# The last sequence's score comparison on GpSimd and ScalarE, and the last block's output in two halves

## The chip, the cores and the metric

The kernel runs on one core of one Trainium2 chip. The metric is the device time of one execution in microseconds. Three runs of the kernel before took 418.65, 418.74 and 420.13 us; the median is 418.74. One more execution was taken by the profiler: it took 417.93 us, of which 416.2 us are the span from the first instruction to the last. All times "at" a moment below are us from the start of that span.

## What is computed

Two layers over a batch of 4 sequences of 1024 rows of 128 numbers. Each layer computes `x = x + s * silu(g)` from the layer-normed `x`. In layer 0, `s` is a decayed linear attention and `g` a four-layer feed-forward network. In layer 1, `s` is a selective state space (a convolution, a gated scan over time with 16 states for each of the 128 channels, a projection) and `g` a mixture-of-depths network, which only the half of the rows with the highest router scores goes through:

```python
# layer 1, s
h = A_discrete[None] * h + xc_t[:, :, None] * B_t[:, None, :]
y = jnp.einsum('bn,bdn->bd', C_t, h) + D_param * xc_t
...
y = y * silu(gate)
y = y @ W_out + b_out
# layer 1, g
k = int(S * CAPACITY_FACTOR)                      # 512 of 1024
top_scores, top_idx = jax.lax.top_k(scores, k)
weights = jax.nn.sigmoid(top_scores)
...
output = jax.vmap(scatter_one)(hidden_states, top_idx, update)
```

The kernel has no sort: it counts for each row how many rows beat it, and keeps the rows that fewer than 512 beat.

## The kernel before

The rows are worked on in 8 blocks of 512 (`NBK`), two to a sequence, with the 128 channels in the partitions. A block goes through the stages `ln0`, `retention`, `gated`, `hidden1`, `hidden2`, `out0` (layer 0), then `ln1`, `front`, `states`, `gates`, `router`, `moe`, `scans`, `project` (layer 1). When both blocks of a sequence have their scores, `ranks(b)` runs for the sequence and `finish(j)` for each of its blocks.

Nothing is issued in the order in which it is written. Every instruction is recorded with a modelled cost and a priority (`TIMES` gives each stage of each block a start), and a list planner, `Plan.order`, decides the order of each engine once, before the launch. `Plan.issue` (line 373) then emits everything, so that line stands at every instruction of the profile and groups are told apart by tile names. On the chip each engine runs its list in that fixed order: an instruction whose input is late holds up all behind it on its engine. SyncE's list (SP in the profile) issues all DMAs.

The steps that the change touches:

- `scans` (lines 921 to 956). For each of 8 double tiles `u` of a block (128x2x512): two DMAs fetch rows of `xd` into `u`; VectorE (DVE) multiplies by `B` (128x1024) and runs two scans (128x512 each); GpSimd (POOL) multiplies by `Cr` (line 950; the very last tile on VectorE); TensorE (PE) sums the states with `sel` into `py`. Tiles are named `u_block_k`; in the last block they come in the order u_7_0, u_7_8, u_7_1, u_7_9, u_7_2, u_7_10, u_7_3, u_7_11, and the first two get their rows from TensorE (`pu`, four products) in place of DMAs. The tag `u` has 6 buffers (line 422).
- `ranks` (lines 891 to 919). For each of 8 chunks `q`, VectorE compares the scores `sc` from that chunk on (n = 1024, 896, ... 128 columns) with the chunk's own scores `col` and adds up the results in the same instruction (lines 907 to 909); a second one, `eq` (line 910), settles ties. TensorE sums `cmp` and `eq` over the partitions into `rank` (lines 911 to 915). `cmp` and `eq` have two buffers each, so chunk q + 2 waits until TensorE has read chunk q. `wm` (router weight or 0) comes out at the end and scales `ff` in `finish`.
- `project` (lines 958 to 969). VectorE makes `y` from `py`, `xc` and `gate`; TensorE multiplies by `W_out`, chunk by chunk, and adds the bias last; ScalarE (ACT) copies the sum `pyo` to `so`.
- `finish` (lines 971 to 982). ScalarE scales `ff`, GpSimd adds `xn`, ScalarE applies silu; then `so * ff`, `x +` that, and the store. In the last block VectorE does the last two.
- The weights `w12_t` (line 591, used by `gated`) and `h_t` (line 596, used by `hidden1` and `hidden2`) have memory of their own to the end.

Of the kernel before, what the change touches and what calls it, by code (L numbers as in the profile page):

```python
# [47 lines left out]
for _name, _w in (  # L48
# [9 lines left out]


TIMES = {  # L60
    "ln0": (10.465, (-34.463, 37.568, 0.307, -8.702, 29.140, 25.837, -0.706, 2.276)),
    "retention": (7.697, (19.747, 29.540, 0.054, 5.261, 0.588, -0.481, 27.669, 17.510)),
    "gated": (0.198, (17.080, -12.778, -2.899, 37.127, 52.075, 3.684, 35.848, 24.681)),
    "hidden1": (181979.521, (10.669, -0.997, 0.654, 26.140, 49.753, 13.692, 29.323, 21.440)),
    "hidden2": (104.604, (6.706, 7.824, 35.607, 17.363, 7.255, 8.335, 12.787, 23.305)),
    "out0": (0.269, (-10.144, 10.621, 13.685, 32.888, 37.354, 6.208, 14.587, 34.725)),
    "ln1": (0.086, (-3.447, -9.822, 3.389, 39.108, 24.646, 10.527, 7.924, 19.641)),
    "front": (99775.310, (31.104, -7.375, 49.241, 35.721, 3.625, 15.911, 8.435, 28.268)),
    "states": (1929558528.870, (-22.925, -12.719, -2.927, -2.692, -1.385, 5.843, 8.364, 33.960)),
    "gates": (2802.502, (-10.124, -3.354, -1.683, 3.017, 7.752, 67.130, 11.212, 9.313)),  # L70
    "router": (35.459, (32.003, 36.047, 1.039, 23.096, 29.397, 12.314, 55.205, 9.245)),
    "moe": (0.850, (-6.037, 10.367, -2.942, 3.023, 8.714, 12.982, 45.904, 32.432)),
    "ranks": (3.658, (7.924, -5.386, 32.363, 0.750, 18.387, 5.771, 15.184, 9.739)),
    "scans": (0.083, (26.879, 6.452, 3.058, 25.041, 26.277, 9.568, 13.774, 14.948)),
    "project": (0.218, (-2.585, 1.221, 6.521, 8.046, 9.527, 12.283, 10.650, 21.658)),
    "finish": (2311.973, (10.042, -1.800, 14.285, 18.479, 29.156, 18.433, 18.474, 24.699)),
    "load_x": (0.107, (32.705, -1.570, 6.609, 55.729, 2.835, 7.712, 33.265, 51.716)),
}
SWITCH = 0.725
SPARE = 2  # L80
XB = 5
BY_PE = (0, NBK - 1)
U_BY_PE = (NBK - 1,)
# [298 lines left out]
def tile_kernel(  # L382
# [34 lines left out]
    for name, n in {  # L417
        "x": XB, "stat0": 2, "ve0": 2, "rs0": 2, "tm0": 2, "stat1": 2, "ve1": 2, "rs1": 2, "tm1": 2, "col": 2, "wm": 2, "most": 2, "eq": 2,
        "nxt": 2, "xn0": 2, "xnT": 1, "qT": 1, "vd": 1, "sT": 1, "st": 1, "y": 1,
        "sc": 1, "xh0": 2, "xl0": 2, "sO": 2, "xh1": 2, "xl1": 2, "Br": 1, "Cr": 2, "bc": 1,  # L420
        "gate": 2, "xc": 2, "cmp": 2, "a": 3, "xn1": 3, "ff": 3, "so": 3,
        "hh": 8, "hl": 8, "h2": 5, "u": 6, "last": 2,
    }.items():
        early = name in ("a", "h2")
        plan.tag(sb, name, n, early or name in ("hh", "hl", "u"), 1 if early else None)

    def tile_(tag, name, shape=(P, HB), dtype=F32):
        if tag == "const":
            tag = name
            plan.tag(sb, tag, 1)  # L430
        return plan.tile(tag, shape, dtype, name)
# [108 lines left out]
    def v(name, i=0, n=P):  # L540
        a = _VEC[name][0] + i
        return vec[0:n, a : a + 1]
# [5 lines left out]
    def c(name):  # L548
        a, b = _CST[name]
        return cs[:, a:b]  # L550
# [3 lines left out]
        return rw[:, a:b].repeat(n)  # L554

    ident = c("ident")
    ones_bf = tile_("const", "ones_bf", (P, 1), BF)
    do("gpsimd", "memset", ones_bf, 1.0, cost=0.05)
    zero = tile_("const", "zero", (P, 3))
# [28 lines left out]
    mm(pM, wqk[:, 0:D], wqk[:, D : 2 * D], True, True)  # L588
    M = split(pM, "M", (P, D))
    place(0.0)  # L590
    w12_t = tile_("const", "w12_t", (P, 2 * F), FR)
    vcopy(w12_t, w12_s)
    place(0.3)
    h_t = []
    for i, s in enumerate(h_s):
        h_t.append([tile_("const", f"h{i}_t{k}", (P, F), FR) for k in range(KC)])
        for k in range(KC):
            vcopy(h_t[i][k], s[k])
    place(0.5)
# [39 lines left out]
    two = tile_("const", "two", (P, P), FR)  # L639
    vcopy(two, two_s[:, 0:P])  # L640

    def add_bias(dst, i):

        mm(dst, two, bias[:, i * D : (i + 1) * D].repeat(CB), False, True)


    wr_s = tile_("sT", "wr", (P, P))
# [243 lines left out]
    def ranks(b):  # L891

        sc, col = prev["sc"], prev["col"]
        wm = tile_("wm", f"wm_{b}", (P, NCH))

        act(AF.Tanh, wm, col, scale=0.5)
        vts(wm, wm, 0.5, 0.5, ALU.mult, ALU.add)


        rank = mm_tile(f"rank_{b}", (P, NCH))  # L900
        most = tile_("most", f"most_{b}", (P, NCH))
        for q in range(NCH):
            n = L - q * P
            cmp = tile_("cmp", f"cmp_{b}_{q}", (P, L), BF)
            eq = tile_("eq", f"eq_{b}_{q}", (P, P), BF)
            cq = col[:, q : q + 1]
            do("vector", "tensor_scalar", cmp[:, 0:n], sc[:, q * P : L], cq, float(TOPK - n),
               op0=ALU.is_le, op1=ALU.add, accum_out=most[:, q : q + 1],
               cost=(n + 66) / 960 + 0.065)
            stt(eq, sc[:, q * P : (q + 1) * P], cq, tie, ALU.is_equal, ALU.mult)  # L910
            with fused("tensor", 0.027 * (NCH - q)):
                for i in range(q + 1, NCH):
                    mm(rank[:, i : i + 1], cmp[:, (i - q) * P : (i - q + 1) * P], ones_bf,
                       q == 0 and i == 1, False)
                mm(rank[:, q : q + 1], eq, ones_bf, False, q == NCH - 1)
        vtt(most, rank, most, ALU.is_lt)
        vtt(wm, wm, most, ALU.mult)
        for g in range(NH):
            R[b * NH + g]["wm"] = wm[:, g * CB : (g + 1) * CB]

    def scans(j):

        b, g = divmod(j, NH)
        xc, xd, Bp, Cr = (R[j][k] for k in ("xc", "xd", "B", "Cr"))
        py = tile_("py", f"py_{j}")
        last = prev.get("last")
        if not g:
            prev["last"] = tile_("last", f"last_{j}", (P, NSC))
        for m in range(4):
            us = []  # L930
            for q in range(0, 4, 2):
                ks = [4 * q + m, 4 * (q + 1) + m]
                u = tile_("u", f"u_{j}_{ks[0]}", (P, 2, HB))
                if m == 0 and j in U_BY_PE:
                    for i, k in enumerate(ks):
                        pu = mm_tile(f"pu_{j}_{k}")
                        mm(pu, rep[q + i], xc, True, True)
                        vtt(u[:, i, :], pu, R[j]["Br"], ALU.mult)
                else:
                    for i, k in enumerate(ks):  # L940
                        dma(u[:, i, :], xd[k * E : (k + 1) * E, :].whole(NS), 0.63, 2.24e5)
                    vtt(u, u, Bp.repeat(2), ALU.mult)
                for i, k in enumerate(ks):
                    do("vector", "tensor_tensor_scan", u[:, i, :], A[:, k : k + 1].bcast(HB),
                       u[:, i, :], last[:, 4 * m + q + i : 4 * m + q + i + 1] if g else 0.0, ALU.mult, ALU.add,
                       cost=(2 * HB + 104) / 960)
                if not g:
                    copy(prev["last"][:, 4 * m + q : 4 * m + q + 2], u[:, :, HB - 1])

                (vtt if j == NBK - 1 and m == 3 and q else ptt)(u, u, Cr.repeat(2), ALU.mult)  # L950
                us += [u[:, 0, :], u[:, 1, :]]
            with fused("tensor", 1.0):
                for q in range(4):
                    mm(py[32 * q : 32 * (q + 1), :], sel[:, 32 * m : 32 * (m + 1)], us[q],
                       m == 0, m == 3)
        R[j]["py"] = py

    def project(j):
        py = R[j]["py"]
        y = tile_("y", f"y_{j}")  # L960
        stt(py, R[j]["xc"], v("Dp"), py, ALU.mult, ALU.add)
        vtt(y, py, R[j]["gate"], ALU.mult)
        po = mm_tile(f"pyo_{j}", (P, CB, D))
        with fused("tensor", 1.15):
            for i, t in enumerate(chunk):
                mm(po[:, i, :], y[:, t], wout_t, i == 0, False)
            add_bias(po, 0)
        R[j]["so"] = so = tile_("so", f"so_{j}", (P, CB, D))
        copy(so.flat(), po.flat())

    def finish(j):
        b, g = divmod(j, NH)
        ff, xn, so, wm = (R[j][k] for k in ("ff", "xn1", "so", "wm"))
        for i in range(CB):
            act(AF.Copy, ff[:, i, :], ff[:, i, :], scale=wm[:, i : i + 1])
        ptt(ff, ff, xn, ALU.add)
        act(AF.Silu, ff, ff)
        xg = xts[j]
        tt = vtt if j == NBK - 1 else ptt
        tt(so, so, ff, ALU.mult)  # L980
        tt(xg, xg, so, ALU.add)
        dma(out[b, g * HB : (g + 1) * HB, :].rearrange("(c p) d -> p c d", p=P), xg)


    def stage(f, j, arg):
# [101 lines left out]
```

## Time and profile before

| | us |
|---|---|
| median of three runs (418.65 to 420.13) | 418.74 |
| the profiled execution | 417.93 |
| its span, first to last instruction | 416.2 |
| VectorE busy in the span | 354.4 |
| GpSimd busy | 288.1 |
| ScalarE busy | 276.3 |

The page of the profile gives busy times of the engines, then the span in 40 slices, then the chain of work that ended last, then the costliest groups. A timeline row reads: start, duration, engine, line, operation, output tile <- input tiles, shape, count; in brackets how long the engine had been idle before it and what ended that. "PEld" is TensorE's weight load, "SPq" a DMA's issue on SyncE's queue. A row with x4 covers four instructions in a row; instructions of VectorE overlap a little, so four scans of 1.26 us take 4.80.

The last block's work in order, from the timeline: `xc` of block 7 (convolution and silu) is written by ScalarE at 363.17 to 363.86. VectorE finishes the scans of block 6 at 366.1, does `ranks` of the last sequence from 366.01 on, and begins block 7's `u` at 374.73. TensorE's last product of the mixture network ends at 391.6. The page's 40 slices of 10.4 us each (busy share in tenths; the last row is the granted TensorE clock in tenths of full speed); the last five cover this stretch:

```
PE   1999999999999999999999999999999999989843
DVE  5594605996999968989999969999999999999992
ACT  3687895876557857875867598668577656772600
POOL 3066542198486897869996488967788898773890
PEclk9999999999999999999999999999999999998966
```

### The profile page before, as it was taken

To read this page: it belongs to the slowest core of one execution; us is meant where nothing else is said; L and a number is where in the kernel's file an instruction comes from. 1 tells how busy PE (TensorE), PEld (TensorE's weight loads), DVE (VectorE), ACT (ScalarE), POOL (GpSimd) and SP (SyncE) were. 2 spreads that over 40 slices of the span, in tenths; PEclk is the share of its full clock that TensorE was granted. 3 is DMA by queue.
4 is the path that set the end of the run, shared out by engine and by line. 5 is a ranking of instruction groups with operands and counts; after the bars stand their busy time and mean duration, and the time that the engine had idled before them with its cause. 6 is when DMAs were issued, how large, how long until landed. Compare 5 with 4: busy or idle time off the path is not lost.

```text
span 416.2 us, 6589 instructions
## 1 busy us (share of the span) xinstructions
PE 389.7 (94%) x2294; PEld 291.1 (70%) x2294; DVE 354.4 (85%) x621; ACT 276.3 (66%) x487; POOL 288.1 (69%) x200
## 2 busy tenths in 40 slices
PE   1999999999999999999999999999999999989843
PEld 1878878866777778777687688677877687747501
DVE  5594605996999968989999969999999999999992
ACT  3687895876557857875867598668577656772600
POOL 3066542198486897869996488967788898773890
PEclk9999999999999999999999999999999999998966
DMA  6900009206418053573602490456073553517300
GB/s 214 330 30 1 2 25 248 57 10 156 120 51 255 27 158 102 133 199 105 202 3 54 132 252 2 116 165 160 1 228 101 158 127 104 125 56 198 103 25 25
DMA packets 37897, 47.44 MB, mean 114 GB/s; under 512 B 7844, under 2 KB 17700, under 8 KB 37864
## 3 DMA queue, kind: packets, MB, share of 16 engines
q1 hardware_dynamic: 37864, 47.02, 40.8%
q8 instruction: 18, 0.29, 0.3%
q14 instruction: 15, 0.12, 0.1%
HBM read 42.40 MB, written 4.60 MB: 113 GB/s over the span
## 4 chain that ended last, share of the span: by engine, by line
PE 82%; DVE 5%; ACT 5%; POOL 4%; issue 2%; DMA 1%; POOLq 1%; SPq 1%; DVEq 0%; ACTq 0%
PE pb L373 15%; PE pa L373 12%; PE p L373 7%; PE py L373 7%; PE pg L373 6%; PE px L373 5%; PE pmo L373 5%; PE pm L373 4%; DVE u L373 4%; PE po L373 3%; POOL u L373 3%; PE pyo L373 2%; PE pv L373 2%; PE psc L373 2%; PE tr L373 2%
## 5 line engine op out<-in xcount | busy, mean ns | idle before, releaser
L373 POOL TENSOR_TENSOR u<-u,Cr 128x1024 f32<-128x1024 f32 x63 | 149.7, 2389 | 31.1 <-ACT last L373 13.0
L373 DVE TENSOR_TENSOR u<-u,B 128x1024 f32<-128x1024 f32 x62 | 73.5, 1206 | 17.1 <-DMA u<-xd 8.7
L373 DVE TENSOR_TENSOR_SCAN u<-bankA,last,u 128x512 f32<-128x512 f32 x64 | 78.5, 1266 | 0.2
L373 DVE TENSOR_TENSOR_SCAN u<-bankA,u 128x512 f32<-128x512 f32 x64 | 74.8, 1207 | 0.4
L373 POOL TENSOR_TENSOR h_l<-a,h_h 128x512 fp32r<-128x512 f32 x32 | 40.9, 1293 | 26.6 <-ACT h_h L373 26.6
L373 ACT ACT_TABLE_LOAD x39 | 50.0, 1283 | 13.6 <-PE pg L373 5.8
L373 POOL TENSOR_TENSOR g_l<-ga,g_h 128x512 fp32r<-128x512 f32 x32 | 40.6, 1293 | 20.5 <-ACT g_h L373 20.5
L373 PE MATMUL pa<-h_h,h_t 128*128 128x512 f32 x128 | 49.6, 405 | 0.0
L373 PE MATMUL pa<-h_l,h_t 128*128 128x512 f32 x128 | 48.6, 397 | 0.0
L373 PE MATMUL pb<-g_h,h_t 128*128 128x512 f32 x128 | 47.3, 396 | 0.0
L373 PE MATMUL pb<-g_l,h_t 128*128 128x512 f32 x128 | 47.1, 395 | 0.1
L373 PE MATMUL py<-u,sel 128*32 128x512 f32 x256 | 40.0, 633 | 7.2 <-POOL u L373 7.2
L373 ACT ACTIVATE h<-pb,vec 128x512 f32<-128x512 f32 x32 | 20.6, 688 | 18.1 <-PE pb L373 16.4
L373 PEld LDWEIGHTS pmo<-W_t,hm 128*128 128x128 f32 x256 | 31.1, 192 | 1.9 <-ACT ff L373 0.8
L373 PE MATMUL pmo<-W_t,hm 128*128 128x128 f32 x256 | 31.5, 275 | 0.0
L373 PEld LDWEIGHTS pg<-w_t,h 128*128 128x128 f32 x256 | 29.9, 192 | 1.0 <-ACT h L373 0.3
L373 PE MATMUL pg<-w_t,h 128*128 128x128 f32 x256 | 30.1, 275 | 0.1
L373 ACT ACTIVATE xn<-x,tm,rs 128x128 f32<-128x128 f32 x64 | 26.9, 486 | 4.6 <-DVE tm L373 4.6
L373 PEld LDWEIGHTS pa<-h_h,h_t 128*128 128x128 f32 x128 | 23.9, 188 | 7.5 <-issue 1.1
L373 PEld LDWEIGHTS pb<-g_h,h_t 128*128 128x128 f32 x128 | 23.9, 188 | 7.0 <-ACT g_h L373 1.3
L373 PEld LDWEIGHTS pa<-h_l,h_t 128*128 128x128 f32 x128 | 24.1, 188 | 6.4 <-POOL u L373 0.8
L373 PEld LDWEIGHTS pb<-g_l,h_t 128*128 128x128 f32 x128 | 23.9, 188 | 6.6 <-POOL g_l L373 1.4
(170 smaller groups left out, 838.3 us busy)
## 6 DMA issues: line engine op xcount, KB each, us to landing
u<-xd SPq DMA_DIRECT2D x124, 256.0 KB, 4.6
x<-in_x_dram SPq DMA_DIRECT2D x8, 256.0 KB, 2.9
xd<-xc SPq DMA_DIRECT2D x8, 256.0 KB, 2.0
out_dram<-x SPq DMA_DIRECT2D x8, 256.0 KB, 3.6
Br<-bd SPq DMA_DIRECT2D x6, 256.0 KB, 4.3
Cr<-bd SPq DMA_DIRECT2D x6, 256.0 KB, 5.6
h_s<-in_h1T_dram SPq DMA_DIRECT2D x4, 256.0 KB, 5.5
h_s<-in_h2T_dram SPq DMA_DIRECT2D x4, 256.0 KB, 4.2
```

The source lines that it names most:

```text
L373: i = getattr(getattr(self.nc, eng), method)(*map(real, args), **{k: real(a) for k, a in kw.items()})
```

## The change

It has four parts.

1. In `ranks` of the last sequence alone, GpSimd compares and ScalarE adds up the results; a constant tile `room`, written by GpSimd at the start, holds what the sum was offset by before, and VectorE adds it once. `eq` stays on VectorE.
2. Five of the last block's eight `u` tiles move (`LAST_U`): u_7_0, u_7_8 and u_7_11 keep the tag `u`; u_7_1 gets the memory of `w12_t`, and u_7_9, u_7_2, u_7_10 and u_7_3 that of `h_t`, whose eight tiles become four double ones.
3. In `project` the bias is added first, not last. The last block works in two halves of 256 columns, and has no copy to `so`.
4. In `finish` of the last block VectorE multiplies straight from the two `pyo` halves and stores each half with a DMA of its own.

`TIMES` gets other numbers, from which the planner makes the order anew.

```diff
-    "ranks": (3.658, (7.924, -5.386, 32.363, 0.750, 18.387, 5.771, 15.184, 9.739)),
+    "ranks": (3.659, (-7.417, -5.314, -1.815, 0.676, 15.725, 5.766, 50.787, 11.656)),
...
+RANKS_BY_POOL = (NB - 1,)
+LAST_U = ("u", "u", "w12", "hw", "hw", "hw", "hw", "u")
...
-        "hh": 8, "hl": 8, "h2": 5, "u": 6, "last": 2,
+        "hh": 8, "hl": 8, "h2": 5, "u": 6, "last": 2, "w12": 1, "hw": 4,
...
+    room = tile_("const", "room", (P, NCH))
+    for q in range(NCH):
+        do("gpsimd", "memset", room[:, q : q + 1], float(TOPK - (L - q * P)), cost=0.05)
...
-    w12_t = tile_("const", "w12_t", (P, 2 * F), FR)
+    w12_t = tile_("w12", "w12_t", (P, 2 * F), FR)
...
-        h_t.append([tile_("const", f"h{i}_t{k}", (P, F), FR) for k in range(KC)])
+        pairs = [tile_("hw", f"h{i}_t{k}", (P, 2, F), FR) for k in range(KC // 2)]
+        h_t.append([pairs[k // 2][:, k % 2, :] for k in range(KC)])
...
-        mm(dst, two, bias[:, i * D : (i + 1) * D].repeat(CB), False, True)
+        mm(dst, two, bias[:, i * D : (i + 1) * D].repeat(dst.shape[1]), first, not first)
...
-            do("vector", "tensor_scalar", cmp[:, 0:n], sc[:, q * P : L], cq, float(TOPK - n),
-               op0=ALU.is_le, op1=ALU.add, accum_out=most[:, q : q + 1],
-               cost=(n + 66) / 960 + 0.065)
+            if b in RANKS_BY_POOL:
+                do("gpsimd", "tensor_scalar", cmp[:, 0:n], sc[:, q * P : L], cq, None,
+                   op0=ALU.is_le, cost=0.2 + n * 0.001)
+                do("scalar", "activation", cmp[:, 0:n], cmp[:, 0:n], AF.Copy,
+                   accum_out=most[:, q : q + 1], cost=(n + 112) / 1200 + 0.19)
+            else:
+                do("vector", "tensor_scalar", cmp[:, 0:n], sc[:, q * P : L], cq, float(TOPK - n),
+                   op0=ALU.is_le, op1=ALU.add, accum_out=most[:, q : q + 1],
+                   cost=(n + 66) / 960 + 0.065)
...
+        if b in RANKS_BY_POOL:
+            vtt(most, most, room, ALU.add)
...
-                u = tile_("u", f"u_{j}_{ks[0]}", (P, 2, HB))
+                home = LAST_U[2 * m + q // 2] if j == NBK - 1 else "u"
+                u = tile_(home, f"u_{j}_{ks[0]}", (P, 2, HB))
...
-        po = mm_tile(f"pyo_{j}", (P, CB, D))
-        with fused("tensor", 1.15):
-            for i, t in enumerate(chunk):
-                mm(po[:, i, :], y[:, t], wout_t, i == 0, False)
-            add_bias(po, 0)
+        n = CB // 2 if j == NBK - 1 else CB
+        R[j]["po"] = po = [mm_tile(f"pyo_{j}_{h}", (P, n, D)) for h in range(0, CB, n)]
+        for h, p in zip(range(0, CB, n), po):
+            t = slice(h * P, (h + n) * P)
+            stt(py[:, t], R[j]["xc"][:, t], v("Dp"), py[:, t], ALU.mult, ALU.add)
+            vtt(y[:, t], py[:, t], R[j]["gate"][:, t], ALU.mult)
+            with fused("tensor", 0.23 * (n + 1)):
+                add_bias(p, 0, True)
+                for i in range(n):
+                    mm(p[:, i, :], y[:, chunk[h + i]], wout_t, False, i == n - 1)
...
-        copy(so.flat(), po.flat())
+        if n == CB:
+            copy(so.flat(), po[0].flat())
...
+            for h in range(0, CB, CB // 2):
+                t = slice(h, h + CB // 2)
+                vtt(so[:, t, :], R[j]["po"][2 * h // CB], ff[:, t, :], ALU.mult)
+                vtt(xg[:, t, :], xg[:, t, :], so[:, t, :], ALU.add)
+                dma(to[:, t, :], xg[:, t, :])
```

The planned order of each engine differs little until block 7's convolution: a few neighbouring instructions change places, and on TensorE the gate product of block 6 and the score product of block 6 stand later among the mixture products of block 5. From there the orders differ. VectorE after its scans of block 6: eq 0 and 1, u_7_0 (two products with `B`, two scans), u_7_8 with the `py` and `y` of block 6 among it, eq 2 before its last scan and eq 3 behind it, the products u_7_1 and u_7_9, eq 4 and 5, scans of u_7_1, eq 6 and 7, scans of u_7_9, then u_7_2 and u_7_10 with the end of `ranks` between their scans, u_7_3 and u_7_11, and the last block's halves. GpSimd: cmp 0 and 1, u_7_0, cmp 2 and 3, u_7_8, cmp 4 and 5, `so` of block 5, cmp 6 and 7, u_7_1, `x` of block 5, u_7_9, u_7_2, u_7_10, `ff` of blocks 7 and 6, u_7_3, `so` and `x` of block 6. TensorE: behind the convolution the gates of blocks 6 and 7, py_6, `B`, `C`, the four `pu`, then the mixture products of blocks 6 and 7 with the `rank` products between them. SyncE: the twelve `u` loads stand straight behind the store of `xc`, and the store of block 5's rows behind them; before, it stood ahead.

## The prediction

> **What bounds the kernel now.** First the page: who is busy, and who stands on the chain that ended last.
>
> ```profile
> PE 389.7 (94%) x2294; PEld 291.1 (70%) x2294; DVE 354.4 (85%) x621; ACT 276.3 (66%) x487; POOL 288.1 (69%) x200
> PE 82%; DVE 5%; ACT 5%; POOL 4%; issue 2%; DMA 1%; POOLq 1%; SPq 1%; DVEq 0%; ACTq 0%
> ```
>
> Over the whole span TensorE sets the time. But the planned order moves little before block 7's convolution (px, 359.92 to 362.73), and TensorE's products are the same ones. So I read the end alone, by a table of stages. Columns: stage, its length, then busy us (instructions) of PE, PEld, DVE, ACT, POOL, granted TensorE clock, DMA share, GB/s.
>
> ```profile
> 365.00:370.00 5.00, 4.88 (x33) 2.29 (x31) 5.00 (x11) 4.60 (x8) 4.52 (x3) 1.00 0.10 35
> 370.00:375.00 5.00, 3.54 (x30) 2.31 (x27) 5.00 (x17) 2.79 (x4) 2.30 (x2) 0.88 0.31 70
> 375.00:380.00 5.00, 5.00 (x19) 2.50 (x17) 4.17 (x10) 1.25 (x2) 0.00 (x0) 0.78 1.06 278
> 385.00:390.00 5.00, 5.00 (x37) 3.75 (x36) 5.00 (x5) 4.90 (x9) 2.98 (x3) 1.00 0.02 5
> 395.00:400.00 5.00, 1.30 (x6) 0.19 (x4) 5.00 (x6) 0.63 (x1) 5.00 (x4) 0.77 0.00 0
> 400.00:405.00 5.00, 3.00 (x8) 0.38 (x8) 4.90 (x5) 0.00 (x0) 4.72 (x3) 0.50 0.17 52
> ```
>
> The reader sees VectorE full from 365 to 405 but for 0.93 us (0.83 and 0.10), while TensorE has slack from 390 on and GpSimd is empty from 375 to 380. The end is VectorE's. The timeline shows with what.
>
> ```profile
> 366.01 1.25 DVE L373 TENSOR_SCALAR_CACHE_REDUCE cmp<-sc,col 128x1024 bf16<-128x1024 f32 x1
> 367.19 0.34 DVE L373 SCALAR_TENSOR_TENSOR eq<-sc,col,bankA 128x128 bf16<-128x128 f32 x1
> 367.45 1.14 DVE L373 TENSOR_SCALAR_CACHE_REDUCE cmp<-sc,col 128x896 bf16<-128x896 f32 x1
> 372.96 5.01 SPq L373 DMA_DIRECT2D u<-xd  x8
> 385.79 4.80 DVE L373 TENSOR_TENSOR_SCAN u<-bankA,last,u 128x512 f32<-128x512 f32 x4
> 404.62 1.23 DVE L373 TENSOR_TENSOR u<-u,Cr 128x1024 f32<-128x1024 f32 x1
> ```
>
> What an instruction costs on a full engine is its pitch, start to next start: cmp 0 takes 367.19 - 366.01 = 1.18, eq 367.45 - 367.19 = 0.26, a scan 1.18 ((4.80 - 1.26) / 3). The last row of VectorE's queue ends at 405.85. After that the tail is a chain with nothing beside it:
>
> ```profile
> 407.87 0.75 DVE L373 SCALAR_TENSOR_TENSOR py<-xc,vec,py 128x512 f32<-128x512 f32 x1 [2.03 <-PE py L373]
> 408.65 0.69 DVE L373 TENSOR_TENSOR y<-py,gate 128x512 f32<-128x512 f32 x1
> 410.83 0.59 ACT L373 COPY so<-pyo 128x512 f32<-128x512 f32 x1 [14.82 <-PE pyo L373]
> 411.45 0.69 DVE L373 TENSOR_TENSOR so<-so,ff 128x512 f32<-128x512 f32 x1 [2.10 <-ACT so L373]
> 412.18 0.69 DVE L373 TENSOR_TENSOR x<-x,so 128x512 f32<-128x512 f32 x1
> ```
>
> **What the comparison takes off VectorE.** Eight pitches from start to start: 1.18, 1.06, 0.94, 0.79, 0.67, 0.53, 0.40, 0.28, together 5.85 us. The eight eq stay. Added: one 128x8 addition, pitch 0.08 as `most` (378.65 to 378.73).
>
> **What it puts on GpSimd.** The trace has no wide one-input instruction there. Its nearest rows:
>
> ```profile
> L373 POOL TENSOR_TENSOR u<-u,Cr 128x1024 f32<-128x1024 f32 x63 | 149.7, 2389 | 31.1 <-ACT last L373 13.0
> L373 POOL TENSOR_TENSOR h_l<-a,h_h 128x512 fp32r<-128x512 f32 x32 | 40.9, 1293 | 26.6 <-ACT h_h L373 26.6
> 1.30 0.53 POOL L373 MEMSET two_s<- 128x512 f32 x1
> ```
>
> Two inputs: (2389 - 1293) / 512 = 2.14 ns a column and 0.2 us an instruction. No input: with the 128x256 memset at 0.31, (0.53 - 0.31) / 256 = 0.86 ns. A comparison reads one tensor, so it lies between; it has one stream less than the first and one more than the second, and I take 1.0 ns, nearer the memset since the second read looks like what is dear. For 4608 columns and 8 x 0.2: 6.2 us; bounds 5.6 and 11.5.
>
> The Trainium skill (GPSIMD Engine Reference, § 4.1 Engine selection) speaks against such a move: elementwise work belongs on VectorE, GpSimd being about twice as slow for two inputs, though roughly at line rate for one. The rows agree on two inputs (2389 ns against 1226 for the same product with `Cr` on VectorE); by "twice as slow" the 5.85 us would become 11.7, the upper bound, and the forecast would be the second rival's; by the line rate it would stay as it is.
>
> **On ScalarE**: eight sums. Its scalings of 128x128 cost 0.32 (1.28 for four), silu of 128x512 0.63, so 0.8 ns a column: 4608 x 0.0008 + 8 x 0.22 = 5.4 us, and between nothing and 0.3 each for reading the sum out (VectorE's is 0.08). ScalarE is idle for over half of 370 to 385; what queues behind is the `hm` of blocks 6 and 7, not due soon.
>
> **Where VectorE now waits.** I walk the new order with old durations. The gate product of block 6 moves behind px (three matmuls, 0.7 us), so px and the activation `xc` come 0.6 us sooner, at 363.3; but one transpose of block 7 slips behind eight `pmo` matmuls (0.9), so VectorE's scans of block 6 end as before, about 366.15. Then eq 0, 1 (0.52). `pu` follows `B` and `C` on TensorE at 0.86 each from 364.2 (py_6 first): 366.95, so 0.3 wait. From 367.0 the pitches are: four u products 4 x 0.61, sixteen scans 18.88, three pairs of products 6.72, eq 2 to 7 1.56, py and y of block 6 1.28, small ones 0.30, `Cr` 1.23 with a gap of 0.19: 32.6 us.
>
> The new waits are in eq 2 to 7, each behind TensorE's reading of the eq two before (two buffers). GpSimd begins cmp 0 at 370.15: u_6_11 ahead of it (2.36) waits for ScalarE's copy of `last`, now behind Br, Cr and B of block 7, 367.75. TensorE ends py_6 at 371.3; nine `pm` (0.23 each) to 373.4, rank 0 (0.8) to 374.2, pyo (1.4) 375.6, rank 1 (0.6) 376.2, three `pmo` (0.9) 378.9, rank 2 379.4, rank 3 379.9, two `pm` and a `pmo` 381.2, py_7 382.2, bias and rank 4 382.9, two `pm` and rank 5 383.7. The comparisons, with u_7_0 and u_7_8 (2.36 each) among them, are there in time, cmp 5 at 380.8. Eq 2 to 7 want to start at 374.6, 376.0, 378.8, 379.8, 382.6, 383.3. The waits are 0, 0.3, 0.7, 0.2, 0.45, 0.55; with two short ones for `pu` and py_6 (0.35) 2.55 us. Queued behind a waiting eq are the scans, so this is on the path. VectorE ends at 366.15 + 0.52 + 0.33 + 32.6 + 2.55 = 402.15 against 405.85: **-3.7 us**. GpSimd ends u_7_3 at 401.4 (370.15, 6.2 of comparisons, seven u 16.6, four others 5.0, 3.5 of waits), before VectorE's u_7_11: cover of 0.75 us. Were it gone, each us more on GpSimd would cost one.
>
> **u in dead memory**: nothing by itself. In before the first eight loads issue from 372.96 behind block 5's store, yet VectorE is full; now all twelve issue from about 366 at 0.63 each, landed by 378, before their products. The cover is VectorE's own work; without it the loads would be on the path by their 4.2 us landing. Block 5's store goes behind them and ends long before block 7's. The memsets of `room` (0.1 each) run while VectorE waits for x to 3.58. Bias first and the paired `h_t` issue the same matmuls: nothing.
>
> **The tail in halves.** From the end of py (407.82) to VectorE's end (412.87): 5.05 us. VectorE's slope is (1202 - 682) / 512 = 1.02 ns a column (its two products with `B`, 1024 and 512 wide), so a 256-column half saves 0.26: 0.49 in place of 0.75, 0.43 in place of 0.69. The py halves end at +1.02, y at +1.47 and +1.82; the four matmul pairs of a half take 0.5; so_a 2.2 to 2.6, x_a to 3.05, so_b to 3.45, x_b to 3.9. The copy (0.59 and its handover) is gone, half of `pyo` hidden. **-1.1 us**; bounds -0.3 (eight instructions wait for each other) and -1.5. The stores' landing, 2.3 us, stays.
>
> Sum: -3.7 - 1.1 = -4.8. The profiled execution becomes 413.1, the span 411.4. It stands 0.8 under the median; carried to that, 418.74 - 4.8 = **413.9 us**.
>
> **Rivals.**
> - No new wait: the 2.55 us of waits do not come about (TensorE reaches the ranks earlier). For it: TensorE and ScalarE have slack. Against: `pmo` and py_7 stand ahead of ranks 2 and 4. -2.55 more: 411.4.
> - The comparison costs what two inputs cost, 2.14 ns. eq 4 to 7 then wait for GpSimd (cmp 5 ends at 385.0, not 380.8), VectorE ends at 403.95, 1.9 before the old end; with the tail -3.0: 415.7.
> - The other side: GpSimd becomes the bound. A comparison with a scalar pointer and a bf16 result may be a slow form; the row `rs` (power, 128x4) takes 1.02 us for four columns, so operations there differ a lot. GpSimd from 370.15 on has 23.2 us beside 4.608 us per ns of column rate, then 3.0 for the last py. It decides from 2.7 ns on: 370.15 + 23.2 + 12.5 + 3.0 = 408.9, the old 407.82 and the 1.1 of the tail. At twice the two-input rate, 4.3 ns, it ends 7 us later: 426.
> - The gain is lost: eq waits of 3.7 us more and half the tail's gain, because the granted clock, 0.78 from 375 to 380, falls lower in TensorE's new gaps and the ranks come late. 418.74 - 0.5: 418.
>
> **How the numbers follow.** Forecast 0.45 (412.5 to 415), no wait 0.15, two-input rate 0.22, GpSimd bound 0.12, gain lost 0.06. The first three hold 0.82; the range is from 410.8 (no wait, tail -1.5, and 0.2 for the runs' spread) to 417.6 (two-input rate with a tail of -0.3 and one us more of waits). A measurement of this kernel can tell 0.5% (2.1 us) from no change. Faster by more: 0.45, 0.15 and 0.17 of the 0.22, 0.77. Same: the rest, the lost gain and a little of the GpSimd case, 0.12. Slower: 0.11.
>
> **What would show it.** cmp on GpSimd: 1.2 us for 1024 columns (2.4 in the second rival, 4 or more in the third). VectorE: idle of 2 to 3 us before the eq, with PE as what ended it; GpSimd named there speaks for the second. Last `Cr` product on VectorE to end near 402, 5.05 to 3.9 us in the tail, `u` loads from 366 on. Wrong if TensorE is late before px, if the last py waits for u_7_3, or if ScalarE's sums hold up `hm` and with it `pmo`.

## The result and the profile after

| | before | after | ratio, 95% interval |
|---|---|---|---|
| first comparison, 20 runs each | 418.61 us | 420.74 us | 1.0046 [1.0031, 1.0060] |
| once more (e1_again), 29 and 6 runs | 418.36 us | 420.85 us | 1.0061 [1.0037, 1.0085] |

Forecast was 413.9 us, 4.8 below; measured is 0.0046 x 418.6 = 1.9 us above. The first profiled run of after took 557.96 us at a granted clock of 0.66; it is left out of the ratios and serves only for durations on engines other than TensorE. The lines of after are from e1_again, the same kernel (418.39 us profiled, span 416.6). Its runs fall into two groups, 418.4 to 418.9 and 420.5 to 422.4; the profiled one is of the lower, so its profile cannot show what makes the upper one (see e14_noport). The page's first and fourth part of e1_again:

```profile
PE 391.2 (94%) x2295; PEld 292.5 (70%) x2295; DVE 349.9 (84%) x610; ACT 278.6 (67%) x500; POOL 303.0 (73%) x216
PE 85%; DVE 4%; ACT 3%; POOL 3%; issue 2%; DMA 1%; SPq 1%; DVEq 0%; ACTq 0%; POOLq 0%
```

VectorE did lose work (354.4 to 349.9 us), but GpSimd gained 14.9 (288.1 to 303.0), not 6.2. The stages of the end (same columns as in the prediction):

```profile
375.00:380.00 5.00, 3.94 (x42) 3.62 (x40) 4.21 (x6) 2.67 (x5) 5.00 (x3) 1.00 0.92 240
380.00:385.00 5.00, 2.67 (x23) 2.20 (x22) 1.85 (x4) 2.34 (x5) 5.00 (x4) 0.85 0.01 5
385.00:390.00 5.00, 5.00 (x30) 2.84 (x29) 2.88 (x5) 2.76 (x7) 5.00 (x5) 0.81 0.00 0
395.00:400.00 5.00, 3.20 (x13) 0.43 (x12) 5.00 (x10) 1.66 (x5) 4.67 (x3) 1.00 0.14 43
400.00:405.00 5.00, 1.92 (x4) 0.19 (x4) 5.00 (x5) 3.92 (x8) 5.00 (x4) 0.56 0.00 0
```

The fifth busy number, GpSimd's, was 0.00 from 375 to 380 before; now it is 5.00 in stage after stage, and the idle time has gone over to VectorE (the third): 1.85 of 5 busy from 380 to 385. The groups of GpSimd (count, then busy us, mean ns of one, idle before), and the waits of VectorE (us in total, times, longest), 365 to 410:

```profile
L375 POOL TENSOR_SCALAR cmp<-sc,col 128x1024 bf16<-128x1024 f32 x1 | 2.8, 2843 | 0.0
L375 POOL TENSOR_SCALAR cmp<-sc,col 128x128 bf16<-128x128 f32 x1 | 0.6, 611 | 0.0
```

```profile
DVE eq L375 <- PE rank L375: 6.1, 5, 1.8
PE rank L375 <- ACT cmp L375: 3.9, 5, 1.4
ACT cmp L375 <- POOL cmp L375: 9.3, 7, 2.5
```

A comparison costs (2843 - 611) / 896 = 2.49 ns a column and 0.29 us an instruction. The waits before the eq are 6.1 us where 2.2 were forecast (2.55 with two short waits elsewhere). They name TensorE, which the prediction took as a sign for its walk and against GpSimd. The two rows below lead further: TensorE's counts waited for ScalarE's sums, which are written over `cmp`, and ScalarE for GpSimd's comparisons. The timeline, GpSimd, then VectorE and TensorE:

```profile
370.74 5.35 POOL L375 TENSOR_SCALAR cmp<-sc,col 128x1024 bf16<-128x1024 f32 x2
378.39 4.06 POOL L375 TENSOR_SCALAR cmp<-sc,col 128x768 bf16<-128x768 f32 x2
384.75 2.78 POOL L375 TENSOR_SCALAR cmp<-sc,col 128x512 bf16<-128x512 f32 x2
388.75 1.51 POOL L375 TENSOR_SCALAR cmp<-sc,col 128x256 bf16<-128x256 f32 x2
403.63 2.35 POOL L375 TENSOR_TENSOR u<-u,Cr 128x1024 f32<-128x1024 f32 x1
```

```profile
381.97 0.35 DVE L375 SCALAR_TENSOR_TENSOR eq<-sc,col,bankA 128x128 bf16<-128x128 f32 x1 [1.77 <-PE rank L375]
405.85 1.23 DVE L375 TENSOR_TENSOR u<-u,Cr 128x1024 f32<-128x1024 f32 x1
```

```profile
406.03 3.02 PE L375 MATMUL py<-u,sel 128*32 128x512 f32 x8 [2.83 <-POOL u L375]
407.13 0.19 PEld L375 LDWEIGHTS py<-u,sel 128*32 128x32 f32 x4 [0.91 <-DVE u L375]
```

The second of these rows as it was before:

```profile
405.89 0.19 PEld L373 LDWEIGHTS py<-u,sel 128*32 128x32 f32 x4 [0.93 <-DVE u L373]
```

The eight comparisons take 5.35 + 4.06 + 2.78 + 1.51 = 13.7 us. With them GpSimd is full from 370.74 until u_7_3 ends at 405.98 (0.23 us idle). This reaches the end through the eq: the sixth comparison ends at 384.75 + 2.78 = 387.53, the last eq starts at 388.88, and from there VectorE is full until its last product ends at 407.08. TensorE's last sum begins behind u_7_3, but the weights of its second half are loaded when VectorE's last product is done, as before, and the sum ends 1.97 us behind that product, as before (405.85 to 407.82, now 407.08 to 409.05). So VectorE is still what the end waits for.

### The profile page after: what moved, and what is told of

It reads as the page before. It is cut to its first block, busy times and chain, and to the rows that moved or that the text cites. A ratio compares the mean times of both kernels' runs of the same rounds, so it can differ in the third digit from the quotient of the medians.

```text
span 556.1 us, 6602 instructions
## 1 busy us (share of the span) xinstructions
PE 534.7 (96%) x2295; PEld 360.2 (65%) x2295; DVE 357.5 (64%) x610; ACT 282.9 (51%) x500; POOL 302.5 (54%) x216
## 4 chain that ended last, share of the span: by engine, by line
PE 93%; DVE 3%; POOL 1%; DMA 1%; issue 1%; ACT 0%; SPq 0%; DVEq 0%; ACTq 0%
PE pb L375 17%; PE pa L375 15%; PE p L375 8%; PE py L375 8%; PE pg L375 8%; PE pmo L375 7%; PE px L375 6%; PE pm L375 5%; PE po L375 4%; PE pyo L375 3%; PE tr L375 2%; PE pv L375 2%; PE psc L375 2%; PE pz L375 2%; PE pq L375 2%; PE pt L375 1%
## 5 line engine op out<-in xcount | busy, mean ns | idle before, releaser
L375 PE MATMUL pa<-h_h,h_t 128*128 128x512 f32 x128 | 63.2, 513 | 0.0
L375 PE MATMUL pa<-h_l,h_t 128*128 128x512 f32 x128 | 62.9, 510 | 0.0
L375 PE MATMUL pb<-g_l,h_t 128*128 128x512 f32 x128 | 61.4, 508 | 0.0
L375 PE MATMUL pb<-g_h,h_t 128*128 128x512 f32 x128 | 61.1, 507 | 0.0
L375 PE MATMUL py<-u,sel 128*32 128x512 f32 x256 | 49.6, 827 | 6.4 <-POOL u L375 6.3
L375 PEld LDWEIGHTS pmo<-W_t,hm 128*128 128x128 f32 x256 | 43.9, 247 | 2.5 <-issue 0.7
L375 PE MATMUL pmo<-W_t,hm 128*128 128x128 f32 x256 | 45.2, 347 | 0.0
L375 PEld LDWEIGHTS pg<-w_t,h 128*128 128x128 f32 x256 | 42.8, 252 | 2.1 <-issue 1.2
L375 PE MATMUL pg<-w_t,h 128*128 128x128 f32 x256 | 43.4, 348 | 0.0
L375 DVE SCALAR_TENSOR_TENSOR a<-p,vec,a 128x512 f32<-128x512 f32 x32 | 24.0, 748 | 21.9 <-PE p L375 10.2
```

What stands on the lines that cost most here:

```text
L375: i = getattr(getattr(self.nc, eng), method)(*map(real, args), **{k: real(a) for k, a in kw.items()})
```

## The experiments

Ratios are to the kernel before on the same chip; one without a ratio was run once.

### The parts alone

e2_halves is before with the halves alone, e3_memory with the u memory alone, e4_no_pool is after without the comparison's move. All three keep the bias first and the paired `h_t`.

```diff
-RANKS_BY_POOL = (NB - 1,)
+RANKS_BY_POOL = ()
...
-LAST_U = ("u", "u", "w12", "hw", "hw", "hw", "hw", "u")
+LAST_U = ("u",) * 8
```

The first edit is in all three, the second in e2_halves; e2_halves and e3_memory have before's `TIMES`, e3_memory before's tail too.

> The changed kernel once more, for a profile at full TensorE clock (the one at hand has a granted clock of 0.66). Theory 1 (the GpSimd comparison is dear): it takes 2.8 us for 1024 columns, 13.7 us for all eight, VectorE idles 4 us or more in front of the eq, the last u of GpSimd ends with or behind VectorE's last; ratio to before 1.002 to 1.007. Theory 2 (the comparison is covered and the rest of the change costs): VectorE is as full as in before from 366 to 405, and the late work stands before px or in the tail.

> Before, with the last block's projection and output in two halves alone (comparison on VectorE, u in its old memory, old start times; bias first). By the prediction's term -1.1 us (bounds -0.3 and -1.5), ratio 0.9974; theory 2, in which the halves cost: +0.5 us or more.

> Before, with the five u tiles of the last block in the memory of dead weights alone (comparison on VectorE, one projection, old start times). By the prediction nothing, within 0.5 us; theory 2, in which the twelve early loads and the delayed store collide with something: +1 us or more.

> The changed kernel with the comparison left on VectorE for all sequences; halves, memory and the new start times stay. Theory 1: -1.1 us against before, and 2.5 to 3.5 us under the changed kernel. Theory 2: no better than the changed kernel, +1 to +3 us against before.

Measured: e1_again 1.0061; e2_halves 0.9978 [0.9966, 0.9990]; e3_memory 1.0010 [0.9997, 1.0022]; e4_no_pool 1.0004 [0.9982, 1.0026]. Theory 1 holds for the price and the waits, but not in its last sign: GpSimd's last u ends 1.1 us before VectorE's. The halves are the only part that gains, 0.9 us, although the pairs cost this kernel too 1 us (see "A loss far ahead of the change"). e4_no_pool was expected 1.1 us under before and came out 0.2 above (-0.8 to 1.1); the pairs can account for 1.0 of that. From e4_no_pool to after lies the comparison's move, with the order that the planner made for it: 1.0061 - 1.0004 = 0.0057, 2.4 us lost (by the two intervals, 1.0 to 3.8) where 3.7 were to be won. (e4_no_pool's runs also fall into two groups, 416.6 to 417.9 and 419.6 to 420.2. Its profiled run, 419.92, is of the upper; the step on `wm` takes 0.52 us there, so the long wait for GpSimd described below is not what makes these groups. What does is open.)

The tail in TensorE's and VectorE's rows of e1_again, then of e2_halves:

```profile
410.63 1.23 PE L375 MATMUL pyo<-wout_t,y 128*128 128x128 f32 x4 [1.06 <-DVE y L375]
```

```profile
411.96 0.42 DVE L375 TENSOR_TENSOR so<-pyo,ff 128x256 f32<-128x256 f32 x1 [1.06 <-PE pyo L375]
```

```profile
409.77 0.71 PE L375 MATMUL pyo<-wout_t,y 128*128 128x128 f32 x4 [1.06 <-DVE y L375]
```

```profile
410.59 0.42 DVE L375 TENSOR_TENSOR so<-pyo,ff 128x256 f32<-128x256 f32 x1 [0.54 <-PE pyo L375]
```

From the last py on VectorE to its end before takes 5.00 us (407.87 to 412.87), e2_halves 4.01, after 4.73. Most of the difference between the latter two is the first half's projection, 0.71 against 1.23 us: the granted clock is 0.74 from 410 to 415 in e2_halves, 0.50 in after. A tail in one piece is on record at that clock too: e18_bias (below) takes 5.68 us with 0.50 from 405 to 415. So at like clocks the halves save about 1.0 us, 5.00 - 4.01 and 5.68 - 4.73, each from one profile. Behind VectorE's end the span goes on for 3.3 us before, 2.7 in e2_halves, 2.8 in after: a store of half the rows also lands sooner.

### Is it the price of a comparison?

In e11_rate2 GpSimd compares 4, 3, 3, 2, 2, 2, 1 and 1 chunks of 128 columns, 2304 of 4608. (The expectations of e11_rate2 and e9_rate say 3, 3, 2, 2, 2, 1, 1, 1 and 1920; the code and the rows below have 2304.) The counts read compared chunks again in place of the rest, and ScalarE sums the compared columns alone. It builds on e10_room2 below, which differs from after only in where `room` lies.

```diff
+            k = (2 * (NCH - q) + 4) // 5 * P if b in RANKS_BY_POOL else n
...
-                do("gpsimd", "tensor_scalar", cmp[:, 0:n], sc[:, q * P : L], cq, None,
+                do("gpsimd", "tensor_scalar", cmp[:, 0:k], sc[:, q * P : q * P + k], cq, None,
...
-                do("scalar", "activation", cmp[:, 0:n], cmp[:, 0:n], AF.Copy,
+                do("scalar", "activation", cmp[:, 0:k], cmp[:, 0:k], AF.Copy,
...
-                    mm(rank[:, i : i + 1], cmp[:, (i - q) * P : (i - q + 1) * P], ones_bf,
+                    c_ = min(i - q, k // P - 1) * P
+                    mm(rank[:, i : i + 1], cmp[:, c_ : c_ + P], ones_bf,
```

> The kernel of e10_room2 in which GpSimd compares only 1920 of the 4608 columns (as in e9_rate; the last sequence's choice of rows is not the reference's). The comparisons cost about 8 us in place of 13.7, against the 6.2 of the prediction. Theory (the comparison's price is the step that failed): 413.5 to 415.5 us, ratio 0.988 to 0.993, eq waits of 0.5 to 2.5 us. Rival (the eq waits come from TensorE's order or clock): ratio 0.996 to 1.000.

Measured 413.02 us, 0.9870 [0.9846, 0.9894]. Its comparisons on GpSimd, and what VectorE waited for:

```profile
371.60 2.79 POOL L375 TENSOR_SCALAR cmp<-sc,col 128x512 bf16<-128x512 f32 x2
376.72 2.14 POOL L375 TENSOR_SCALAR cmp<-sc,col 128x384 bf16<-128x384 f32 x2
381.17 1.83 POOL L375 TENSOR_SCALAR cmp<-sc,col 128x256 bf16<-128x256 f32 x2
384.22 1.20 POOL L375 TENSOR_SCALAR cmp<-sc,col 128x128 bf16<-128x128 f32 x2
```

```profile
DVE eq L375 <- PE rank L375: 0.5, 1, 0.5
```

Together 7.96 us, 5.74 less than in after; the waits at the eq fall from 6.1 to 0.5. From the start of the comparisons to the end of the last sum: after 370.74 to 409.05, here 371.60 to 404.13, 5.78 us less. It can be split. From the start of the comparisons to the end of the sixth, GpSimd takes 16.79 us in after (370.74 to 387.53) and 11.40 here (371.60 to 383.00): 5.4 us. From there to the last eq it is 1.35 us in after and 0.88 here (383.00 to 383.88): 0.5 us, in which lie ScalarE's shorter sum (0.52 and 0.42 us for the sixth) and TensorE's clock (0.81 from 385 to 390 in after, 1.00 from 380 to 390 here). TensorE's order is the same in both. So the price of the comparisons is the cause of 5.4 of the 5.8 us; ScalarE and the clock have 0.5 at most. The time is a little below what was expected, and close to the prediction's 413.9.

An earlier attempt, e9_rate, did the same on e5_room, whose copy of `room` stood at the start and pushed two exponentials behind other activations: 39 table loads in place of after's 37 (before has 39 too, without that delay), and TensorE 4.6 us later by block 0's gate products (42.49 against 37.85). All three kernels with it carry that.

> The kernel of e5_room in which GpSimd compares only the first 3, 3, 2, 2, 2, 1, 1, 1 chunks of 128 columns of the eight comparisons (1920 of 4608 columns; sums and counts read compared chunks twice in place of the others, so the last sequence's choice of rows is not the reference's). At 0.29 us and 2.5 ns a column the comparisons then cost 7.1 us, near the 6.2 that the prediction took. Theory (the comparison's price is what failed, and the rest of the walk holds): 413.5 to 415.5 us, ratio to before 0.988 to 0.993, eq waits of 2 to 3.5 us. Rival (the eq wait for TensorE's order or its clock whatever the comparison costs): eq waits stay near 6 us, 417 to 418.5, ratio 0.996 to 1.000.

> The kernel of e5_room with five more buffers for `eq` in the last sequence, so that VectorE never waits for TensorE's reading of an earlier eq (6.06 us of such waits in after's trace). Theory (GpSimd is a second bound just behind: full from 370.7, its last product u_7_3 ends at 405.98, 1.1 us before VectorE's last): the waits move from the eq to the end of the scans and the gain is at most 1.1 us against e5_room, a ratio to before of 0.997 to 1.000; VectorE's or TensorE's last wait names GpSimd. Rival (the eq waits alone are the loss): 4 to 6 us less than e5_room, ratio 0.987 to 0.991.

e9_rate came to 419.16 us (1.0013), 4.1 us late at block 0's gate: less that, 415.1, inside the theory's bounds; its eq waits were 0.5 us, fewer than expected. e6_eqz came to 427.83 us (1.0215), 1.7 above e5_room, where the theory had a small gain and the rival a large one: VectorE still waited 3.7 us at the eq, and 2.1 for ScalarE's sums, which waited for the comparisons. A third loss, 3.96 us at one small instruction, is the subject of the next part but one; what more buffers would bring without it is not shown.

### What GpSimd charges for an instruction

> Before with instructions added behind its last ones, GpSimd's on 128x1024 f32: comparisons (pointer to bf16, pointer to f32, constant to bf16), multiplication by a pointer and by a constant, a copy, an addition of two tensors. Theory A (what one input costs there is a rate of its own, whatever the operand or the result): all five one-operand forms 2.4 to 2.9 us. Theory B (the pointer or the bf16 result is dear): the constant or the f32 result comes at 1.0 to 1.5 us. Behind them twelve VectorE additions of 128x4 run beside one GpSimd addition of about 2.4 us, once with an operand in PSUM and once with both in SBUF. Port theory: the first twelve take 1.0 to 1.6 us, while in the second twelve one lasts 1.5 to 2.4 us and ends with GpSimd's. Rival: both twelve alike.

The added rows on GpSimd of e7_forms (`j_` names; `j_pt` is a pointer, without it the operand is a constant):

```profile
413.72 2.86 POOL L1003 TENSOR_SCALAR j_bf<-j_src,j_pt 128x1024 bf16<-128x1024 f32 x1 [8.75 <-DVE j_pt L1003]
416.56 2.85 POOL L1003 TENSOR_SCALAR j_dst<-j_src,j_pt 128x1024 f32<-128x1024 f32 x1
419.39 2.77 POOL L1003 TENSOR_SCALAR j_bf<-j_src 128x1024 bf16<-128x1024 f32 x1
425.07 2.77 POOL L1003 TENSOR_SCALAR j_dst<-j_src 128x1024 f32<-128x1024 f32 x1
427.91 1.04 POOL L1003 COPY j_dst<-j_src 128x1024 f32<-128x1024 f32 x1
429.03 1.89 POOL L1003 TENSOR_TENSOR j_dst<-j_src 128x1024 f32<-128x1024 f32 x1
```

Theory A holds: the pointer adds 0.08 us, the bf16 result nothing, and it does not matter whether it compares or multiplies (425.07). Only the copy runs at the 1.0 ns a column that the prediction took; an operation with one tensor and one scalar takes 2.77 to 2.86 us, more than an addition of two tensors (1.89, both inputs the same tensor) and more than the kernel's product with `Cr` (2.37). The Trainium skill (GPSIMD Engine Reference, § 4.1 Engine selection) has one input at roughly line rate on GpSimd: true of the copy (1.04 us for 1024 columns), not of this form; the measurement decides.

The same run's two times twelve small additions on VectorE beside GpSimd's addition (ns: least, median, most):

```profile
L1003 DVE TENSOR_TENSOR j_d<-j_a,bankA_j x12: 148/157/159, 431.2 to 433.3; 128x4 f32<-128x4 f32 x12
L1003 DVE TENSOR_TENSOR j_d<-j_a,j_b x12: 161/162/1496, 433.5 to 437.0; 128x4 f32<-128x4 f32 x12
```

With one operand in PSUM none takes over 159 ns (the twelve take 2.26 us, not the 1.0 to 1.6 expected), though GpSimd runs its 1.89 us addition for most of them. With both in SBUF one takes 1496 ns: it starts at 433.52, and GpSimd's addition ends at 433.11 + 1.89 = 435.00.

### Three small instructions that wait for GpSimd

In the first profile of after, `most + room` on VectorE, and GpSimd's work beside it:

```profile
533.50 2.40 DVE L375 TENSOR_TENSOR most<-most,room 128x8 f32<-128x8 f32 x1
```

```profile
531.19 4.68 POOL L375 TENSOR_TENSOR u<-u,Cr 128x1024 f32<-128x1024 f32 x2
```

128x8 elements take 2.40 us, to the end of GpSimd's second product (535.87). In e1_again the same row took 0.16: it fell into the moment between two products (396.18). And in e6_eqz the weight's first step, one input but SBUF to SBUF, stood through two products (398.79 to 403.49):

```profile
399.56 3.96 DVE L375 TENSOR_SCALAR wm<-wm 128x8 f32<-128x8 f32 x1
```

The Trainium skill (GPSIMD Engine Reference, § 1 Specifications) says that GpSimd shares its SBUF interfaces with VectorE, and that it contends with VectorE instructions that have two SBUF inputs or run in a two-port mode. The rows with two SBUF inputs agree; whether the step on `wm`, which has one, ran in a two-port mode no trace shows. In the first profile VectorE stood until the product beside it had ended, in e6_eqz until the next one had ended too. Three runs tested whether this makes after's upper group of times.

```diff
-            vtt(most, most, room, ALU.add)
+            vtt(most, most, room_in_psum, ALU.add)
...
-        vts(wm, wm, 0.5, 0.5, ALU.mult, ALU.add)
+        vts(half_in_psum, wm, 0.5, 0.5, ALU.mult, ALU.add)
...
-        vtt(wm, wm, most, ALU.mult)
+        vtt(wm, half_in_psum, most, ALU.mult)
```

Here `room_in_psum` and `half_in_psum` stand for two slices of the PSUM tile `bankA`. e5_room and e10_room2 have the first edit, e14_noport all three.

> After with one edit: a copy of `room` is kept in PSUM, so that `most + room` reads one operand from SBUF and one from PSUM. Theory (VectorE's small addition of two SBUF tiles is held until GpSimd's running product ends, 2.40 us in one profile of after and 0.16 in the other, where it fell between two products): the addition takes 0.1 to 0.2 us in every run, the runs lie closer together than after's 418.4 to 422.4, and the ratio to before is 0.999 to 1.002. Rival (the spread of after's runs is the clock's): no change, 1.003 to 1.007 with the same spread.

> After, with the copy of `room` in PSUM made at another place, so that the exponentials at the start stay where they were (in e5_room their move put two more table loads and 4.6 us into the first 30 us) and every engine's order is after's but for that one copy. Port theory: `most + room` no longer waits for GpSimd; its row takes 0.1 to 0.2 us, the runs lie closer together than after's, the ratio to before is 0.998 to 1.003 (after: 1.0046 and 1.0061). Rival: the spread is the clock's, 1.003 to 1.007.

> The kernel of e10_room2 in which the weight's first step (`wm` times 0.5 plus 0.5, 128x8, SBUF to SBUF) also writes to PSUM and the last step reads it there, so that none of the three small instructions between VectorE's last scans is of the form that waited for GpSimd in a trace (`wm` 3.96 us in e6_eqz, ended with GpSimd's two products). Order as in after. Port theory (these rows, and not the clock, make two groups of after's runs, near 418.5 and near 421): all runs within 1.2 us of 418.5, ratio 0.999 to 1.002. Rival (the groups come from elsewhere, such as TensorE's clock): groups and ratio 1.004 to 1.006 remain.

e5_room: 426.12 us (1.0170), 4.6 us of it at the start, and another planned order at the end, so it decides nothing here. e10_room2: 420.90 us, 1.0046 [1.0024, 1.0069], runs from 418.3 to 422.0 like after's: the theory failed in this form. Right ahead of `most`, `wm` could still wait; its one trace, of a run in the lower group (418.32), has 0.14 us there and does not show it. e14_noport: 419.29 us, 1.0008 [0.9995, 1.0020], and 11 of 12 runs lie between 419.18 and 419.43 (before on this chip: 418.96): the two groups are gone. Its rows on VectorE, then GpSimd's beside them:

```profile
396.80 0.17 DVE L375 TENSOR_SCALAR bankA<-wm 128x8 f32<-128x8 f32 x1
397.08 0.16 DVE L375 TENSOR_TENSOR most<-most,bankA 128x8 f32<-128x8 f32 x1
```

```profile
394.29 4.84 POOL L375 TENSOR_TENSOR u<-u,Cr 128x1024 f32<-128x1024 f32 x2
```

Both now run while GpSimd is in the second of its products. 1.0046 - 1.0008 = 0.0038: keeping these operands in PSUM took 1.6 us off after's mean (0.8 to 2.4). That it was the wait is argued from the 2.40 and 3.96 us above; no run of after's upper group was profiled at full clock.

### A loss far ahead of the change

From block 0's first gate product (pg) to block 7's, TensorE took 302.44 us before and 303.38 in e1_again. All traces at full clock of kernels that hold the pairs showed it, 303.34 to 303.55.

```diff
-        h_t.append([tile_("const", f"h{i}_t{k}", (P, F), FR) for k in range(KC)])
+        pairs = [tile_("hw", f"h{i}_t{k}", (P, 2, F), FR) for k in range(KC // 2)]
+        h_t.append([pairs[k // 2][:, k % 2, :] for k in range(KC)])
```

e17_pairs is before with this alone, e18_bias before with the bias first alone, e16_own the best version (below) without it.

> Before with the paired `h_t` alone. Theory: from pg of block 0 to pg of block 7 303.3 to 303.5 us. Rival: 302.4 us.

> Before with the bias first in every `project`, alone. Theory (the pairs cost the 0.95 us): from pg of block 0 to pg of block 7 302.4 us. Rival (bias first costs it): 303.3 to 303.5 us.

Measured: e17_pairs 303.54 us (38.97 to 342.51), e18_bias 302.37 (38.20 to 340.57), e16_own 302.46. The pairs cost 1.0 us, bias first nothing. TensorE's products with `h_t` in `hidden2`, in e17_pairs, then in e18_bias, over the whole span:

```profile
L373 PE MATMUL pb<-g_h,h_t 128*128 128x512 f32 x128 | 47.8, 400 | 0.1
L373 PE MATMUL pb<-g_l,h_t 128*128 128x512 f32 x128 | 47.6, 398 | 0.0
```

```profile
L373 PE MATMUL pb<-g_h,h_t 128*128 128x512 f32 x128 | 47.3, 396 | 0.0
L373 PE MATMUL pb<-g_l,h_t 128*128 128x512 f32 x128 | 47.1, 395 | 0.1
```

The same 128 products with the same operands take 400 ns for 396, and 398 for 395; those of `hidden1` take 1 ns more. Why tiles in pairs are slower was not tried. (e3_memory, which holds pairs, measured only +0.4 us with an interval from -0.1 to 0.9; whether the u memory gives a little back was not separated.)

### A version that beats both

e12_split is e2_halves with chunks 2 to 7 of the comparison on GpSimd and 0 and 1 left on VectorE; e13_odd moves chunks 1, 3, 5, 7. The planner gets the measured price, and ScalarE adds the offset itself, so that `room` is gone, and writes to `junk` in place of `cmp`. Against after, without the extra `eq` buffers:

```diff
+POOL_CHUNKS = (2, 3, 4, 5, 6, 7)
...
-            if b in RANKS_BY_POOL:
+            if b in RANKS_BY_POOL and q in POOL_CHUNKS:
                 do("gpsimd", "tensor_scalar", cmp[:, 0:n], sc[:, q * P : L], cq, None,
-                   op0=ALU.is_le, cost=0.2 + n * 0.001)
-                do("scalar", "activation", cmp[:, 0:n], cmp[:, 0:n], AF.Copy,
-                   accum_out=most[:, q : q + 1], cost=(n + 112) / 1200 + 0.19)
+                   op0=ALU.is_le, cost=0.2 + n * 0.0026)
+                do("scalar", "activation", junk[:, 0:n], cmp[:, 0:n], AF.Copy,
+                   bias=(TOPK - n - 0.5) / n, accum_out=most[:, q : q + 1], cost=(n + 112) / 1200 + 0.3)
```

> A version meant to beat both: the kernel of e2_halves, with chunks 2 to 7 of the last sequence's comparison on GpSimd (2688 of 4608 columns, 8.3 us by after's rows) and chunks 0 and 1 on VectorE; the planner is given the measured 2.6 ns a column; ScalarE's sum adds the offset itself and writes elsewhere, so that TensorE need not wait for it and `room` is gone; five more eq buffers. VectorE loses pitches of 0.94, 0.79, 0.67, 0.53, 0.40, 0.28: 3.61 us. Theory (8.3 us fit into the time in which GpSimd stood idle before, 372.4 to 380.15, so that no new wait takes the gain): 414 to 415.5 us, ratio 0.988 to 0.994. Rival (at 2.6 ns a column any share of the comparison is lost on GpSimd): ratio 0.997 or more, no better than e2_halves.

> The kernel of e12_split with chunks 1, 3, 5, 7 on GpSimd (2048 columns, 6.4 us) and two eq buffers: VectorE and GpSimd compare at the same time. VectorE loses 1.06, 0.79, 0.53, 0.28: 2.66 us. Theory: 414.5 to 416 us, ratio 0.990 to 0.995. Rival: waits for GpSimd between VectorE's own comparisons, ratio 0.997 or more.

> The kernel of e12_split with the eight `h_t` tiles in memory of their own again, as in before (its u tiles do not use that memory); every engine's order is e12_split's. In the traces the time from the first gate product of block 0 (pg) to that of block 7 is 302.44 and 302.40 us for the code of before, and 303.34 to 303.51 in all nine traces with after's code, growing by about 0.03 us at single pa and pb products. Theory (the paired `h_t` costs this 0.95 us): 302.4 us between the two, ratio to before 0.985 to 0.989 beside e12_split's 0.9893. Rival (bias first, or another of after's common edits): 303.4 us, ratio as e12_split.

The three theories hold, and the rivals do not. Measured: e12_split 413.94 us, 0.9893 [0.9868, 0.9917]; e13_odd 415.28, 0.9908 [0.9879, 0.9936]; e16_own 412.82, **0.9863 [0.9834, 0.9893]**, 5.7 us under before. The intervals of e12_split and e16_own overlap; that the pairs cost them 1 us is seen in the trace (302.46 against 303.51). GpSimd's comparisons in e12_split, and two stages:

```profile
371.06 4.08 POOL L376 TENSOR_SCALAR cmp<-sc,col 128x768 bf16<-128x768 f32 x2
375.52 3.69 POOL L376 TENSOR_SCALAR cmp<-sc,col 128x512 bf16<-128x512 f32 x3 [0.39 <-ACT junk L376]
381.51 0.61 POOL L376 TENSOR_SCALAR cmp<-sc,col 128x128 bf16<-128x128 f32 x1
```

```profile
375.00:380.00 5.00, 4.28 (x40) 3.66 (x39) 5.00 (x6) 4.34 (x12) 4.61 (x5) 1.00 0.50 159
380.00:385.00 5.00, 5.00 (x35) 4.33 (x34) 5.00 (x6) 2.62 (x7) 5.00 (x4) 1.00 0.01 2
```

8.4 us of comparisons fill what was GpSimd's gap, and VectorE stays full: no eq wait is left. GpSimd waits 0.39 us for ScalarE at 375.52, and 1.07 for VectorE's `wm` at 392.79. Against e2_halves the move brings 0.9978 - 0.9893 = 0.0085, 3.6 us (2.4 to 4.7), for 3.61 us taken off VectorE.

## Why the prediction failed, step by step

- **What bounds the end: right.** VectorE was full and GpSimd empty from 375 to 380. The last sum ends 1.97 us behind VectorE's last product in before, after and e11_rate2 alike, and e12_split gained 3.6 us where 3.61 were taken off VectorE.
- **What it takes off VectorE: right in kind.** VectorE is 4.5 us less busy over the span, for 5.85 that the comparison was to take off.
- **"I take 1.0 ns, nearer the memset": the step that failed.** The price is 2.49 ns and 0.29 us an instruction, 13.7 us for 6.2, beyond even the upper bound of 11.5. The bound rested on the thought that one tensor can't cost more than two; e7_forms shows that it can.
- **The waits of 2.55 us** became 6.1 at the eq for that reason: "the comparisons are there in time, cmp 5 at 380.8" no longer held, cmp 5 ended at 387.53. The walk also gave no time to ScalarE's sum between a comparison and its count (0.31 to 1.06 us each). The walk with the measured waits, and VectorE's start on the ranks 0.9 us later than assumed, gives 402.15 + 0.9 + 3.6 = 406.7, beside 407.08 measured. This is the way of the second rival, eq that wait for GpSimd, at a price above its own.
- **e11_rate2 reached 413.0 where 413.9 had been forecast, in part by luck.** Its comparisons still take 1.8 us more than 6.2 and the pairs cost 1.0 us that no term had, but its eq waits are 0.5 us, not 2.2: the walk had too much for these.
- **The cover of 0.75 us on GpSimd** held: u_7_3 ends 1.1 us before VectorE's last product (405.98 and 407.08). The third rival's sum with the measured price, 370.15 + 16.6 + 5.0 + 13.7 + 3.0 = 408.45, lies near the measured 409.05, but by coincidence: the last sum waits for u_7_3 in its first half alone, as before, and for VectorE in its second.
- **u in dead memory: no gain found**, as forecast (e3_memory); the twelve loads are issued from 366.21, as the walk had it.
- **"Bias first and the paired `h_t` issue the same matmuls: nothing": half wrong.** Bias first costs nothing, the pairs 1.0 us: the same instructions are not the same durations.
- **The tail, -1.1:** VectorE's part is -0.3 in after and -1.0 in e2_halves. The step is about right at like clocks (-1.0); it had no term for the clock, 0.50 in after's tail. The store lands 0.5 to 0.6 us sooner, which the step had denied. -0.8 in all for after.
- **Not seen at all: the one added addition.** It was priced at 0.08 us from `most`, which has an operand in PSUM; `room` and `wm` do not. With these in PSUM the mean is 1.6 us lower (e14_noport).
- The range's upper end adds up to 417.5 (418.74 - 1.9 - 0.3 + 1.0), not 417.6; nothing hangs on it.

Sum, in us: the last sum against block 7's gate, +0.4 in place of -3.7 (409.05 - 341.23 = 67.82 against 407.82 - 340.37 = 67.45); the pairs +0.95; the waits of small instructions +1.6; the tail -0.8: +2.1, beside +1.9 measured. The agreement is closer than the terms are known: they come from single profiles and one difference of means, and the same stretch to the last sum takes 66.39 us in e7_forms, whose work up to there is before's, so the first term is known to about 1 us.

## What to carry to other kernels

Price an instruction by a row of its own form: here a copy on GpSimd took 1.04 us, an operation with a scalar 2.77 to 2.86 and one with two tensors 1.89 to 2.37, so the one in between was the dearest. Move as much work as fills the idle time of the engine that takes it: 8.4 us on GpSimd gained, 13.7 lost. When a wait names an engine, ask what that engine waited for. And look where the operands of even a 128x8 instruction lie when two engines may share a path.

## What was not expected of the hardware

- GpSimd: 2.77 to 2.86 us for 128x1024 with one tensor and a scalar, whatever the operation or result, 1.04 for a copy.
- VectorE: a 128x8 instruction stood 2.40 and 3.96 us behind GpSimd's products with both operands, or operand and result, in SBUF; 0.16 and 0.17 with PSUM on one side.
- TensorE: 1 to 4 ns of 400 more per product when `h_t` lies in pairs.
